# Keys' features turned by a trip through DRAM and VectorE's block transpose, and a linear attention's division moved to ScalarE

## The chip, the core and the metric

The kernel runs on one core of a Trainium2 chip. The core has TensorE (PE, with PEld for its weight loads), VectorE (DVE), ScalarE (ACT), GpSimd (POOL) and SyncE (SP), which here issues the DMAs, and 16 DMA engines. The metric is the time of one execution on the device in microseconds (us), as a median over runs. Everything is computed in 32-bit floats.

## What is computed

The input is 16 images of 56 x 56 tokens with 128 channels. There are two layers.

```
x = x + window_attention(group_norm(x))       # shifted windows of 7x7, 4 heads of 32
t = tokens(x)                                 # 16 x 3136 x 128
t = t + linear_attention(layer_norm(t))
t = t + recurrent(layer_norm(t))              # y_t = sigmoid(Wx_t + y_(t-1) V^T)
```

The change lies in the linear attention, which is causal over the 3136 tokens of an image:

```
q, k, v = split(x @ W.T + b);  q = elu(q) + 1;  k = elu(k) + 1
num_t = q_t . sum over s <= t of (k_s outer v_s)
den_t = q_t . sum over s <= t of k_s + 1e-6
out_t = num_t / den_t
```

The recurrence normalises over all images together before it starts, so it begins when everything else is done.

## The kernel before

**Stages.** The first stage, from the start to about 1538 us, does the window attention, the linear attention and the recurrence's input projection of all images. The second runs the recurrence, cut into 32 segments per image.

**Tiles.** An image is eight rows of windows (`window_row`, L830) and seven token groups (`token_group`, L1200): six full groups of 512 tokens in four chunks of 128, and one of 64. That makes 128 rows, 96 full groups and 16 small ones.

**A full group's linear attention.** The layer norm's scale is applied by GpSimd (L1101). The scaled tokens are then turned, channels to partitions, by a trip through DRAM (`through_dram`, L1045): SP issues one write of 256 KB (L1050) and four reads of 64 KB (L1057) into one of four buffers of tag "xp", and VectorE turns blocks of 32 x 32 (L1129). This is done for key "a" (linear attention) and key "f" (recurrence), for all images but the last. TensorE projects to the features of keys and queries (L1259), ScalarE and VectorE make the elu (L1269, L1278, L1287), channels on partitions. The values come out with tokens on partitions (L1312, L1321). The keys' features `f1` are needed in both forms. As they are they enter the products of keys and queries (L1375, masked by L1385). With tokens on partitions, `k`, they enter the running state, so TensorE transposes them chunk by chunk into a PSUM bank (L1335) and ScalarE copies them out (L1339).

**State.** For each chunk TensorE adds keys times values to a PSUM bank that holds the running sums (L1415), and ScalarE copies it (L1427). A chunk's result is queries times the state before it (L1404) plus the masked products times the values (L1407), in a pair of PSUM banks, with the divisor as the last column. VectorE takes the reciprocal of the divisors (L1477, L1480) and does one multiply-add per chunk onto the residual `xt_buf` (L1484). The result is stored (L1184) and goes on to the second layer norm.

**What sets the order.** Every piece of work is a step with an engine, a cost, a rank and the buffers that it takes and drops (`Plan`, L57). A list scheduler simulates all steps, forwards and backwards in 200 passes, keeps the order with the shortest simulated span, and emits the instructions in it. Each engine, and SP as the queue of the DMAs, then works through its own instructions in that order, and semaphores do the waiting. A changed step gives a new order of the whole stage. Buffers that matter here: three PSUM banks "b", two PSUM pairs "a", four buffers "xp", one each of "f0" and "f1", two of "k", three of "state".

**Dormant code.** With `KEYS = ('f', 'a')` (L30) `blocks_moved("k", ...)` (L1041) is false, so the branch at L1354, the strided writes at L1343 and the strided reads at L1350 are not used before the change.

Of the kernel before, what the change touches and what calls it, by code (L numbers as in the profile page):

```python
# [11 lines left out]
AF = mybir.ActivationFunctionType  # L12
ALU = mybir.AluOpType
# [13 lines left out]


TOL2 = 2.0 ** -38
KEYS = ('f', 'a')  # L30


class Buf:
# [201 lines left out]
def tile_conv_attn_hybrid(  # L235
# [19 lines left out]
    nc = tc.nc  # L255
    B, H, W, C = x.shape
    P = 128
# [4 lines left out]
    G = 4  # L262
# [165 lines left out]
    with ExitStack() as s1:  # L428
# [75 lines left out]
        for xt in xt_bufs:  # L504
# [22 lines left out]
                "f1": 1,  # L527
                "k": 2,
                "A": 1,
                "state": 3,  # L530
            }
        )
# [32 lines left out]
        s = issued = plan.step("SP", 0.1, -1.0, lambda: None, lag=19.0)  # L565
# [80 lines left out]
        def part(g, full, mini):  # L646

            return full if g < NG - 1 else mini
# [392 lines left out]
        def blocks_moved(key, b, g):  # L1041

            return key in KEYS and b < B - 1 and g < NG - 1

        def through_dram(key, b, g, src, xp, rank, after, drops):  # L1045

            there = xn_d[key][b, g]

            def away():
                nc.sync.dma_start(  # L1050
                    there.rearrange("s p r -> p s r"),
                    src().rearrange("p (s r) -> p s r", s=4),
                )

            def back():
                for s4 in range(4):
                    nc.sync.dma_start(  # L1057
                        at_spare(xp)[32 * s4 : 32 * (s4 + 1)].rearrange(
                            "i (q r) -> i q r", q=4
                        ),  # L1060
                        there[s4].rearrange("(q i) r -> i q r", q=4),
                    )
# [137 lines left out]
        def token_group(b, g, i, t, turned_x, rows_done, oT_buf, xt_buf, rank):  # L1200


            n = f"{b}_{g}"
            d, df = {}, {}
            st = plan.step
            v1 = v_bufs[i % 2]
            t0, t1 = group_tokens(g)
            nt = t1 - t0
            xg = chunks_of(g, t["xt"])
            np, nk, _ = xg.shape  # L1210
# [21 lines left out]
            def plus_attention():  # L1232
# [10 lines left out]
                takes=[bo],  # L1243
                drops=[oT_buf],
# [4 lines left out]
            xo, scaled = layer_scale(t, g, d, "a", rank, [s], xnT)  # L1249
# [3 lines left out]
            def feature(j):  # L1253
                key = f"f{j}"
                bp, r, f = Buf("b"), Buf("r"), Buf(key)

                def proj():
                    d[f"p{j}"] = bank(bp, P, nt)
                    nc.tensor.matmul(  # L1259
                        d[f"p{j}"],  # L1260
                        awc_sb[:, j * P : (j + 1) * P],
                        d["xT"][:, :nt],
                        start=True,
                        stop=True,
                    )

                def relu():
                    d[f"r{j}"] = own(r, P, GT)[:, :nt]
                    nc.scalar.activation(  # L1269
                        d[f"r{j}"],  # L1270
                        d[f"p{j}"],
                        AF.Relu,
                        bias=bqk_neg[:, j : j + 1],
                        scale=-1.0,
                    )

                def expo():
                    nc.scalar.activation(d[f"r{j}"], d[f"r{j}"], AF.Exp, scale=-1.0)  # L1278

                def larger():  # L1280
                    d[key] = own(f, P, GT)
                    to, a1, a2 = d[key][:, :nt], d[f"p{j}"], d[f"r{j}"]
                    if j and blocks_moved("k", b, g):
                        to = to.rearrange("p (c k) -> p k c", k=G)
                        a1 = a1.rearrange("p (k c) -> p k c", k=G)
                        a2 = a2.rearrange("p (k c) -> p k c", k=G)
                    nc.vector.scalar_tensor_tensor(  # L1287
                        to,
                        a1,
                        bqk_one[:, j : j + 1],  # L1290
                        a2,
                        ALU.add,
                        ALU.max,
                    )
# [10 lines left out]
            def chunk(f, cc):  # L1305
                return f[:, CK * cc : CK * (cc + 1)]
# [41 lines left out]
            def keys(cc):  # L1348
                if blocks_moved("k", b, g):
                    return d["f1"].rearrange("p (c k) -> p k c", k=G)[:, cc]  # L1350
                return chunk(d["f1"], cc)

            bk, k, bA, A = Buf("b"), Buf("k"), Buf("b"), Buf("A")
            if blocks_moved("k", b, g):  # L1354
# [17 lines left out]
            def products():  # L1372
                d["pA"] = bank(bA, P, nk, np)
                for cc in range(nk):
                    nc.tensor.matmul(  # L1375
                        d["pA"][:, cc, :],
                        keys(cc),
                        chunk(d["f0"], cc)[:, :np],
                        start=True,
                        stop=True,  # L1380
                    )
# [97 lines left out]
                d["rd"] = rd[:np, 0:na, 0:ni]  # L1479
                nc.vector.reciprocal(d["rd"], den)  # L1480

            def update():
                for cc in range(nk):
                    nc.vector.scalar_tensor_tensor(  # L1484
                        xg[:, cc, :],
                        d["pn4"][:, cc // 2, cc % 2, 0:C],
                        d["rd"][:, cc // 2, cc % 2 : cc % 2 + 1],
                        xg[:, cc, :],
                        ALU.mult,
                        ALU.add,  # L1490
                    )
# [498 lines left out]
```

## Time and profile before

| | before |
|---|---|
| median of 3 runs | 1694.72 us (1693.42 to 1697.08) |
| the profiled execution | 1699.48 us |
| its span, first to last instruction | 1697.7 us |
| granted TensorE clock, mean | 0.992 |
| recurrence, from about 1538 us on | 160 us |
| DMA packets | 539117, of them 208960 under 512 bytes |

The profile is a page of sections and answers to questions about the trace. Busy time is time in which an engine works, its share is of the span. The chain of work that ended last follows the last instruction back to what released it, step by step. A row of a group reads: line, engine, operation, written tile <- read tiles, shapes, count | busy us, mean ns of one | idle time just before, and what ended it. A DMA's landing is the time from its issue to its last semaphore. Matmuls are pipelined and their ends are modelled, so their durations overlap.

The DMA issues of the trips through DRAM in the page, with KB each and median us to landing:

```profile
xna_d<-spare SPq DMA_DIRECT2D x90, 256.0 KB, 2.5
spare<-xna_d SPq DMA_DIRECT2D x360, 64.0 KB, 2.0
xnf_d<-spare SPq DMA_DIRECT2D x90, 256.0 KB, 2.3
spare<-xnf_d SPq DMA_DIRECT2D x360, 64.0 KB, 2.1
```

The first of each pair is the write and the second the four reads, 90 groups each.

### The profile page before, as it was taken

Reading aid. Unit: us, or ns where it says so; the run is one execution under the profiler, and the core shown is the slowest. Engines: PE = TensorE matmul, PEld = TensorE weight load, DVE = VectorE, ACT = ScalarE, POOL = GpSimd, SP = SyncE. Lnnn points to the kernel's source line nnn. Section 1 sums busy time; section 2 is a strip of 40 time slices with the busy share of each in tenths; the row PEclk is TensorE's granted clock in tenths of the full one; section 3 lists DMA queues with packets and bytes.
Section 4 is the critical chain, followed back from the end, with each engine's and each line's share of the span. In section 5 each row is a group of like instructions: output and inputs, shape, how many; then the busy total and the mean of one; then the engine's idle time right before and its main releaser. Section 6 shows DMA issues by size and latency. Waiting matters only on the chain.

```text
span 1697.7 us, 63511 instructions
## 1 busy us (share of the span) xinstructions
PE 1651.5 (97%) x25819; PEld 1348.0 (79%) x25819; DVE 1444.7 (85%) x3354; ACT 1139.0 (67%) x2846; POOL 1152.5 (68%) x2042
## 2 busy tenths in 40 slices
PE   7999999999999999999999999999999998999997
PEld 6778878888887888888888888888787887786875
DVE  5889988898979898988988898989788876777997
ACT  5667667667676676766766767667666675666765
POOL 6788778688778687877876887787676765651000
PEclk9999999999999999999999999999999999999998
DMA  5465646364545547463746365545543343558999
GB/s 134 102 161 122 173 126 170 103 163 135 154 132 139 129 119 186 116 167 107 182 116 159 114 141 157 151 124 131 143 121 96 102 140 95 163 175 325 405 418 378
DMA packets 539117, 274.81 MB, mean 162 GB/s; under 512 B 208960, under 2 KB 522560, under 8 KB 537024
## 3 DMA queue, kind: packets, MB, share of 16 engines
q1 hardware_dynamic: 537232, 269.89, 54.5%
q8 instruction: 204, 3.34, 0.8%
q10 hardware_dynamic: 1584, 0.79, 0.2%
q14 instruction: 97, 0.79, 0.1%
HBM read 147.94 MB, written 122.65 MB: 159 GB/s over the span
## 4 chain that ended last, share of the span: by engine, by line
PE 81%; DVE 7%; POOL 4%; DMA 3%; issue 3%; SPq 1%; ACT 1%; DVEq 0%; POOLq 0%; ACTq 0%
PE bank L1259 9%; PE bank L857 9%; PE bank L878 6%; PE pair L902 6%; PE pair L957 5%; PE state_bank L1415 5%; PE pair L1404 5%; PE pair L1407 5%; PE pair L976 5%; PE bank L1312 5%; PE bank L1375 5%; PE bank L1224 5%; PE bank L1502 4%; DVE z_buf L1773 3%; PE z_buf L1785 3%
## 5 line engine op out<-in xcount | busy, mean ns | idle before, releaser
L928 POOL TENSOR_TENSOR s<-s,mx 128x784 f32<-128x784 f32 x128 | 192.4, 1503 | 84.9 <-DVE mx L925 82.3
L947 POOL TENSOR_TENSOR p_buf<-p_buf,rc 128x784 f32<-128x784 f32 x128 | 194.6, 1521 | 80.4 <-DVE rc L944 39.7
L1259 PE MATMUL bank<-xnT,awc_sb 128*128 128x512 f32 (+1 forms) x448 | 211.2, 554 | 4.6 <-DVE xt_buf L1233 3.4
L1269 ACT ACTIVATE r<-bank,bqk_neg 128x512 f32<-128x512 f32 (+1 forms) x224 | 142.7, 637 | 101.0 <-PE bank L1259 84.6
L1404 PEld LDWEIGHTS pair<-state,f 128*128 128x128 f32 x768 | 126.1, 191 | 53.5 <-issue 35.9
L1287 DVE SCALAR_TENSOR_TENSOR f<-bank,bqk_one,r 128x512 f32<-128x512 f32 (+1 forms) x224 | 147.6, 659 | 23.2 <-ACT r L1278 10.7
L1407 PE MATMUL pair<-v_buf,A 128*128 128x129 f32 x800 | 155.4, 276 | 0.8 <-issue 0.4
L967 ACT COPY pT<-pair 128x904 f32<-128x904 f32 x128 | 118.1, 923 | 54.6 <-PE pair L957 42.4
L1415 PEld LDWEIGHTS state_bank<-v_buf,k 128*128 128x128 f32 x768 | 123.7, 192 | 38.9 <-issue 21.0
L1415 PE MATMUL state_bank<-v_buf,k 128*128 128x129 f32 x768 | 153.8, 282 | 0.5 <-ACT state L1427 0.2
L1427 ACT COPY state<-state_bank 128x129 f32<-128x129 f32 x384 | 105.2, 274 | 72.7 <-PE state_bank L1415 69.9
L1404 PE MATMUL pair<-state,f 128*128 128x129 f32 x768 | 152.1, 280 | 0.0
L913 DVE TENSOR_TENSOR s<-pair,wmask_sb 128x784 f32<-128x784 f32 x128 | 122.9, 960 | 32.0 <-PE pair L902 27.8
L942 DVE TENSOR_REDUCE sm<-p_buf 128x16 f32<-128x784 f32 x128 | 121.9, 952 | 21.3 <-ACT p_buf L938 21.1
L1213 POOL TENSOR_TENSOR xt_buf<-xt_buf,bout_sb 128x512 f32<-128x512 f32 (+1 forms) x112 | 129.3, 1159 | 14.2 <-DMA xt_buf<-in_x_dram 13.9
L1788 ACT ACTIVATE y_a<-z_buf,bsh 128x256 f32<-128x256 f32 (+1 forms) x218 | 103.3, 474 | 45.5 <-PE z_buf L1785 41.5
L1278 ACT ACTIVATE r<-r 128x512 f32<-128x512 f32 (+1 forms) x224 | 130.7, 584 | 2.5
L902 PEld LDWEIGHTS pair<-kT,q_buf 32*49 32x49 f32 x8192 | 106.3, 121 | 32.3 <-issue 16.3
L1785 PE MATMUL z_buf<-y_a,fvT_sb 128*128 128x256 f32 (+1 forms) x432 | 129.7, 385 | 0.5 <-ACT y_a L1788 0.4
L902 PE MATMUL pair<-kT,q_buf 32*49 32x49 f32 x8192 | 122.6, 206 | 4.8 <-issue 4.8
L957 PEld LDWEIGHTS pair<-ident,p_buf 113*128 113x128 f32 x1024 | 108.1, 142 | 21.6 <-issue 9.6
L1407 PEld LDWEIGHTS pair<-v_buf,A 128*128 128x128 f32 x800 | 121.8, 192 | 3.9 <-issue 1.9
(162 smaller groups left out, 4619.0 us busy)
## 6 DMA issues: line engine op xcount, KB each, us to landing
x_d<-xt_buf SPq DMA_DIRECT2D x96, 256.0 KB, 2.5
xt_buf<-in_x_dram SPq DMA_DIRECT2D x93, 256.0 KB, 3.4
spare<-in_x_dram SPq DMA_DIRECT2D x60, 392.0 KB, 4.7
xs_d<-staged SPq DMA_DIRECT2D x15, 1568.0 KB, 7.0
xna_d<-spare SPq DMA_DIRECT2D x90, 256.0 KB, 2.5
spare<-xna_d SPq DMA_DIRECT2D x360, 64.0 KB, 2.0
xnf_d<-spare SPq DMA_DIRECT2D x90, 256.0 KB, 2.3
spare<-xnf_d SPq DMA_DIRECT2D x360, 64.0 KB, 2.1
```

What stands on the lines that cost most here:

```text
L857: nc.tensor.matmul(d[key], wqkv_sb[:, j * P : (j + 1) * P], xk, start=True, stop=True)
L902: nc.tensor.matmul(sc[64 * hh : 64 * hh + WT, hp, w * WT : (w + 1) * WT], qT[r : r + HD, w * WT : (w + 1) * WT], d["kT"][r : r + HD, w * W ...
L928: nc.gpsimd.tensor_tensor(d["sf"], d["sf"], d["mx"].unsqueeze(2).to_broadcast([P, nb, WT]), ALU.subtract,)
L947: nc.gpsimd.tensor_tensor(prf, prf, d["rc"].unsqueeze(2).to_broadcast([P, nb, WT]), ALU.mult)
L957: nc.tensor.transpose(pt[:, hp, w2, 0:NQ2], pr[0:NQ2, hp, 2 * w2 : 2 * w2 + 2, :].rearrange("p w k -> p (w k)"), ident[0:NQ2, 0:NQ2],)
L1259: nc.tensor.matmul(d[f"p{j}"], awc_sb[:, j * P : (j + 1) * P], d["xT"][:, :nt], start=True, stop=True,)
L1269: nc.scalar.activation(d[f"r{j}"], d[f"p{j}"], AF.Relu, bias=bqk_neg[:, j : j + 1], scale=-1.0,)
L1287: nc.vector.scalar_tensor_tensor(to, a1, bqk_one[:, j : j + 1], a2, ALU.add, ALU.max,)
L1404: nc.tensor.matmul(to, chunk(d["f0"], cc), t["states"][c], start=True, stop=False)
L1407: nc.tensor.matmul(to, d["A"][:, cc, :], v1[:, cc, :], start=c == 0, stop=True)
L1415: nc.tensor.matmul(t["pd"], d["k"][:, cc, :], v1[:, cc, :], start=c == 0, stop=True, skip_group_check=True,)
L1785: nc.tensor.matmul(z, fvT_sb, y_prev, start=False, stop=True, skip_group_check=True)
```

## The change

Two things are changed together.

**Keys.** "k" joins `KEYS`. For 15 images' full groups the keys' features go from `f1` to DRAM and come back. One write stores the tile `f1` (channels on partitions) as four chunks, each 128 x 128. Then four reads, one per quarter of 32 token places, bring for each of 32 partitions 16 runs of 32 numbers, 128 bytes each. VectorE's block transpose then reads and writes the 128 x 512 tile in plain order. The four TensorE transposes and ScalarE's copy of these groups go, and so does their PSUM bank. The strided forms of the dormant code go too.

**Division.** ScalarE multiplies the four chunks by their reciprocals out of PSUM into a new tile `at`. VectorE adds `at` to the residual in one instruction over the group. The pair of PSUM banks is dropped by ScalarE's step instead of VectorE's.

```
-KEYS = ('f', 'a')
+KEYS = ('f', 'a', 'k')
...
+                "at": 1,
...
+            runs = there.rearrange("s (q i) r -> i (s q) r", q=4)
...
             def back():
                 for s4 in range(4):
+                    to = at_spare(xp)[32 * s4 : 32 * (s4 + 1)]
+                    if key == "k":
+                        to = to.rearrange("i (n c) -> i n c", c=32)
+                        part = runs[:, :, 32 * s4 : 32 * (s4 + 1)]
+                    else:
+                        to = to.rearrange("i (q r) -> i q r", q=4)
+                        part = there[s4].rearrange("(q i) r -> i q r", q=4)
+                    nc.sync.dma_start(to, part)
...
             def turn_blocks():
                 d["k"] = own(k, P, G, C)
-                nc.vector.transpose(
-                    d["k"].rearrange("p k (q c) -> p k q c", q=4),
-                    at_spare(xp).rearrange("p (q c k) -> p k q c", q=4, k=G),
-                )
+                nc.vector.transpose(d["k"].rearrange("p k c -> p (k c)"), at_spare(xp))
...
+            def divided():
+                d["at"] = own(at, P, G, C)[:np, :nk]
+                for cc in range(nk):
+                    nc.scalar.activation(
+                        d["at"][:, cc, :],
+                        d["pn4"][:, cc // 2, cc % 2, 0:C],
+                        AF.Copy,
+                        scale=d["rd"][:, cc // 2, cc % 2 : cc % 2 + 1],
+                    )
+
             def update():
-                for cc in range(nk):
-                    nc.vector.scalar_tensor_tensor(
-                        xg[:, cc, :],
-                        d["pn4"][:, cc // 2, cc % 2, 0:C],
-                        d["rd"][:, cc // 2, cc % 2 : cc % 2 + 1],
-                        xg[:, cc, :],
-                        ALU.mult,
-                        ALU.add,
-                    )
+                nc.vector.tensor_tensor(xg, xg, d["at"], ALU.add)
...
-            up = st("DVE", part(g, (1.04, 1.12), (0.26, 0.34)), rank, update, [s, scaled], drops=[apn])
+            at = Buf("at")
+            s = st("ACT", part(g, (0.90, 1.00), (0.22, 0.32)), rank, divided, [s], takes=[at], drops=[apn])
+            up = st("DVE", part(g, (0.60, 0.69), (0.20, 0.28)), rank, update, [s, scaled], drops=[at])
```

More of the change, by code (lines that the diff above doesn't have):

```diff
@@ L1056, in back @@
                 for s4 in range(4):
[L1057 to L1061, printed above, removed]
-                    )
+                    to = at_spare(xp)[32 * s4 : 32 * (s4 + 1)]
[6 more added lines that the diff above has]
+                    nc.sync.dma_start(to, part)
             s = plan.step("SP", 0.7, rank, away, after, drops=drops, lag=2.6)
@@ L1281, in larger @@
                     d[key] = own(f, P, GT)
[L1282 to L1286, printed above, removed]
                     nc.vector.scalar_tensor_tensor(
-                        to,
-                        a1,
+                        d[key][:, :nt],
+                        d[f"p{j}"],
                         bqk_one[:, j : j + 1],
-                        a2,
+                        d[f"r{j}"],
                         ALU.add,
@@ L1342, in turn_blocks @@
                 d["k"] = own(k, P, G, C)
-                nc.vector.transpose(
-                    d["k"].rearrange("p k (q c) -> p k q c", q=4),
-                    at_spare(xp).rearrange("p (q c k) -> p k q c", q=4, k=G),
-                )
[L1348 to L1351, printed above, removed]
+                nc.vector.transpose(d["k"].rearrange("p k c -> p (k c)"), at_spare(xp))
             bk, k, bA, A = Buf("b"), Buf("k"), Buf("b"), Buf("A")
@@ L1376, in products @@
                         d["pA"][:, cc, :],
-                        keys(cc),
+                        chunk(d["f1"], cc),
                         chunk(d["f0"], cc)[:, :np],
@@ L1480, in divisors @@
                 nc.vector.reciprocal(d["rd"], den)
-            def update():
-                for cc in range(nk):
-                    nc.vector.scalar_tensor_tensor(
-                        xg[:, cc, :],
-                        d["pn4"][:, cc // 2, cc % 2, 0:C],
-                        d["rd"][:, cc // 2, cc % 2 : cc % 2 + 1],
-                        xg[:, cc, :],
-                        ALU.mult,
-                        ALU.add,
-                    )
+            def divided():
[7 more added lines that the diff above has]
+                    )
+            def update():
+                nc.vector.tensor_tensor(xg, xg, d["at"], ALU.add)
             s = st("DVE", (0.29, 0.37), rank, divisors, pns)
-            up = st("DVE", part(g, (1.04, 1.12), (0.26, 0.34)), rank, update, [s, scaled], drops=[apn])
+            at = Buf("at")
+            s = st("ACT", part(g, (0.90, 1.00), (0.22, 0.32)), rank, divided, [s], takes=[at], drops=[apn])
+            up = st("DVE", part(g, (0.60, 0.69), (0.20, 0.28)), rank, update, [s, scaled], drops=[at])
             store(b, g, t, up, xt_buf, rank)
```

## The prediction

> **What bounds the kernel now.** I read the page first: the engines' shares, then the chain of work that ended last.
>
> ```profile
> PE 1651.5 (97%) x25819; PEld 1348.0 (79%) x25819; DVE 1444.7 (85%) x3354; ACT 1139.0 (67%) x2846; POOL 1152.5 (68%) x2042
> ...
> PE 81%; DVE 7%; POOL 4%; DMA 3%; issue 3%; SPq 1%; ACT 1%; DVEq 0%; POOLq 0%; ACTq 0%
> ```
>
> TensorE is the busiest engine and holds 81% of the chain; VectorE is next, ScalarE and GpSimd have about a third free. The table by stretches then separates the attention stage (16 to 1538 us) from the recurrence behind it, where GpSimd is nearly idle and the DMA engines are full.
>
> ```profile
> 400.00:700.00 300.00, 298.96 (x5053) 245.79 (x5052) 263.01 (x637) 208.12 (x532) 230.55 (x405) 1.00 0.52 139
> 700.00:1000.00 300.00, 298.83 (x5041) 244.82 (x5040) 263.72 (x634) 205.99 (x523) 232.54 (x409) 1.00 0.54 139
> 1300.00:1538.00 238.00, 228.14 (x3411) 187.19 (x3411) 180.50 (x455) 152.75 (x392) 149.54 (x297) 0.99 0.42 135
> 1538.00:1697.70 159.70, 144.66 (x833) 114.11 (x831) 140.49 (x231) 104.24 (x220) 2.63 (x7) 0.97 0.96 387
> ```
>
> Columns: stretch, length, busy time of PE, PEld, DVE, ACT, POOL, granted clock, DMA share, GB/s. In steady state TensorE is hardly ever idle by this table and VectorE is busy for 88% (263.7 of 300). The change touches only the attention stage. Last, the chain itself, in a stretch around 706 us:
>
> ```profile
> 706.21 0.86 PE bank L1259 x2
> 707.07 0.44 PE bank L1335 x4
> 707.51 0.89 PE bank L1224 x8
> 708.40 0.22 PE pair L1404 x2
> 708.63 0.22 PE pair L1407 x2
> ```
>
> One TensorE step follows the other without a hole, and the four transposes of the keys (L1335) take 0.44 us of it. But the chain is not TensorE everywhere. Near 764 us it runs through a trip to DRAM:
>
> ```profile
> 763.74 1.00 POOL spare L1101
> 764.74 0.03 POOL ld_f L1087
> 764.76 4.14 DMA xna_d<-spare
> 768.90 0.02 issue
> 768.92 0.32 SPq L1057
> ```
>
> So TensorE sets the pace, with exceptions at just the kind of trip of which the change makes more.
>
> **The change, part by part.** Full groups of 512 tokens number 96 (16 images by 6); 90 of them (all but the last image's) send their keys through DRAM.
>
> TensorE loses the four transposes. The chain gives 0.44 us for them, so 90 x 0.44 = 39.6 us, nearly all of it on the path. The group's row has more:
>
> ```profile
> L1335 PE MATMUL bank<-ident,f 128*128 128x128 f32 x384 | 58.5, 274 | 1.9 <-issue 1.9
> L1339 ACT COPY k<-bank 128x512 f32<-128x512 f32 x96 | 56.7, 590 | 25.0 <-PE bank L1335 24.5
> L1484 DVE SCALAR_TENSOR_TENSOR xt_buf<-pair,rd,xt_buf 128x128 f32<-128x128 f32 x384 | 106.1, 339 | 1.1
> L1129 DVE STREAM_TRANSPOSE xnT<-spare 128x512 f32<-128x512 f32 x90 | 63.2, 702 | 14.8 <-DMA spare<-xna_d 12.3 <-PE bank L1259 2.0
> ```
>
> 58.5 us busy over 96 groups is 0.61 us each; the sum by it would be 54.9 us. I take 0.44, because the next step starts that much later (707.07 to 707.51) and the busy time overlaps it. The Trainium skill (Perfetto Trace Analysis, Identifying the Most-Contended Engine) calls matmul busy time a bad measure of how near TensorE is to its limit, since matmuls are pipelined. That agrees with 0.61 beside 0.44 here, and is a warning that the 97% holds small holes. By it the gain would be at most 39.6 us.
>
> ScalarE loses the copy out of PSUM, 90 x 0.59 = 53 us, and gains four scaled copies of 128x128 per full group. That form isn't in the trace; the nearest are the state copy (128x129 from PSUM, 0.274 us) below and the 128x392 scaled copy of the queries (L862, 0.501 us) above. At 0.274 it is 96 x 1.10 = 105 us, plus 16 small groups at about 0.25 = 4 us; at 0.501 it is 196 us. I take the former, whose shape is the same. Net +56 us on an engine busy 1028 us of the stage's 1522: 71%. Nothing, as long as the planner fits them in.
>
> VectorE loses four multiply-adds per group (106.1/96 = 1.11 us) and gains one addition of 128x512: 0.678 us by the residual after the window attention (L1233), 0.692 us by the one scaling with everything in SBUF (L1109). It also gains the block transpose: 0.702 us by L1129, which walks its tile in strides, 0.617 us by the 128x448 of the image (L676), 0.705 for 512 columns. Per group with keys moved: -1.11 + 0.69 + 0.70 = +0.28 us, 90 of them +25; the other six groups -0.42 each, the small ones about nothing. Net +22 us on 1296: VectorE goes from 85% of the stage to 87%, or 88% of a stage 22 us shorter. The row hides it in VectorE's own idle time; without that cover it costs up to 22 us.
>
> The PSUM bank of the transposed keys is freed for about 1 us per group (0.44 + 0.59). TensorE's waits at L1335 itself come to 8.1 us, at L1224 for the keys' copy to 2.2 us. This gain I bound by 0 and 10 us and leave it out of the sum.
>
> DMA and SP gain one write of 256 KB and four reads of 64 KB in 90 groups. The diff's reads are of 32 numbers, 128 bytes: 4 x 512 packets. Two short windows of the DMA view give the price of each kind:
>
> ```profile
> DMA packets 2752, 0.35 MB, mean 141 GB/s; under 512 B 2752, under 2 KB 2752, under 8 KB 2752
> ...
> q1 hardware_dynamic: 2752, 0.35, 88.8%
> ```
>
> This is an image's load in 128-byte runs, 814.0 to 816.5 us: 0.888 x 2.5 us x 16 engines / 2752 = 12.9 ns a packet. At 1425.0 to 1427.5 us a store in 512-byte runs had 481 packets and 32.4%: 26.9 ns. So the keys' read takes 2048 x 12.9 / 16 = 1.65 us of all 16 engines, where the layers' reads take 512 x 26.9 / 16 = 0.86, and the write 0.86 as well. 90 x 2.51 = 226 us on top of 0.51 x 1522 = 776: the DMA share of the stage goes from 51% to 66%. The Trainium skill (DMA: Bandwidth & Descriptors, Specifications) speaks against this part: it wants runs of at least 512 bytes for full rate. The rows show the loss, 1.9 times the time per byte, but at 66% there is still room for it.
>
> SP issues five more DMAs per group: 0.38 us for the write (L1050's median) and 4 x 0.43 (L1057's) = 2.1 us. At each read SP also waits for the write's landing; the queue's own waits give 122.2 + 88.8 = 211 us for the 180 trips of now, 1.17 us each. Together 3.3 us per group, 295 us more. Behind it in SP's order stand the next group's layer trips, the stores and the image loads. The issues at their medians now come to 720 x 0.43 + 180 x 0.38 + 112 x 0.38 + 109 x 0.46 + 60 x 0.50 = 501 us (layer reads, layer writes, stores, loads, image loads), with the landing waits 712, so SP is held 47% of the stage, after the change 66%.
>
> The moved keys come later. Now: 0.44 + 0.59, about 1.0 us after VectorE's maximum. Then: the write's landing 2.5 us, four issues 1.7, the last landing 2.0, transpose 0.7: 6.9 us. The groups come every 1522/96 = 15.9 us, so a planned order can cover the 5.9 us; the single buffers of the two feature tiles and the state chain (L1415, L1427, L1404) bound how far. What waits is VectorE at the block transpose, with everything behind it. Today's 180 transposes waited 24.2 + 12.3 = 36.5 us for their data, 0.20 us each. 90 more at that price are 18 us; at twice the price, because the queues are fuller and the layers' trips lengthen too, 36 us; wholly covered, 0. I take 18, next to the only rows there are.
>
> The planner makes the whole order anew. Of the stage's chain some 206 us are not TensorE (1522 less 81% of 1697.7 plus the 59 us that the recurrence's chain spends on TensorE). A tenth of it either way, 20 us, is my estimate for a luckier or unluckier order.
>
> **Sum.** -39.6 + 18 = -21.6 us. The profiled execution took 1699.48 us, with a span of 1697.7; it lies 4.8 us above the median of 1694.72. So 1677.9 us against its own time and **1673 us** against the median.
>
> **The rivals.**
> 1. All of TensorE's time comes back and the freed bank adds its part: -40 to -50 us, 1645 to 1655. For it: the gapless chain, ScalarE's free third. Against: the 0.20 us per transpose are already seen.
> 2. VectorE becomes the bound, or the reordering eats the gain: -39.6 + 18 + 22 = 0, 1685 to 1702. For it: 88% busy and waits in order. Against: its idle time of 12% is more than the 22 us.
> 3. Slower: the DRAM trips set the pace. One group's three trips share SP; when the keys' part (3.3 us of issue and landing wait) stands before the next layer trip on the chain, that trip is 3.3 us late, as at 764 us where a write of 2.5 us took 4.14. It decides from 39.6 / 3.3 = 12 of the 90 groups on; in 18 groups it costs 59 us and gives 1695 - 40 + 59 = 1714. For it: the chain has trips of 4 us today, and SP goes to 66%. Against: they are few, DMA and SPq being 4% of the chain (68 us).
> That the change does nothing of what it says is out: the transposes do leave TensorE.
>
> **How the numbers follow.** Forecast 0.42, between 1656 and 1690. Rival 1: 0.15. Rival 2: 0.17, a half of it within 0.2% (1691.3 to 1698.1), which is about what a measurement of this kernel can tell from no change, the rest 0.05 faster and 0.04 slower. Rival 3: 0.26. So faster 0.42 + 0.15 + 0.05 = 0.62, same 0.08, slower 0.30. The range reaches from rival 1's low end, 1645, to rival 3 in 18 groups, 1715.
>
> **What would show it.** Right: L1335 and L1339 with only 24 transposes and 6 copies left; TensorE's chain share as high as now in a stage of about 1500 us; the transpose of the keys near 0.70 us, waiting some 20 us for its DMA; VectorE near 88%, DMA share near 0.66 in the steady state. Wrong: TensorE with visible holes that end at L1415 or behind a block transpose; writes to DRAM landing in 4 us instead of 2.5; many more DMA and SPq pieces in the chain; four scaled copies that take far more than 1.1 us and hold the pair of PSUM banks.

## The result: 3.2% slower, and the profile after

The changed kernel takes 1750.05 us (median of 4 runs, 1743.08 to 1753.03) against 1694.51 us before on the same chip: a ratio of 1.032 [1.0287, 1.0352], so 55.5 us more. The forecast was 21.6 us less. The profiled execution took 1750.3 us with a span of 1748.5. Line numbers are those of the changed kernel: L1052 writes a trip's data to DRAM, L1066 reads them back, L1342 is the keys' block transpose, L1133 that of the two layers' tokens, L1406 the product of values and keys into the running sums, L1476 ScalarE's scaled copies, L1484 VectorE's addition. In the kernels that change the keys alone, the numbers around these are lower by one.

The engines' shares and the chain of work that ended last, of the kernel after:

```profile
PE 1644.4 (94%) x25459; PEld 1316.7 (75%) x25459; DVE 1482.2 (85%) x3156; ACT 1188.8 (68%) x3156; POOL 1172.6 (67%) x2042
...
PE 29%; DVE 23%; DMA 20%; SPq 11%; POOL 9%; issue 6%; ACT 2%; DVEq 0%; POOLq 0%
SPq L1066 10%; DMA spare<-xnk_d 5%; DMA xnk_d<-f 4%; PE bank L1263 3%; DMA xna_d<-spare 3%; PE bank L858 3%; DMA spare<-xnf_d 2%; DVE xt_buf L1484 2%; DMA xnf_d<-spare 2%; PE z_buf L1780 2%; PE bank L879 2%; POOL p_buf L948 2%; DVE z_buf L1768 2%; PE bank L1311 2%; DVE f L1286 2%
```

The engines' busy shares hardly moved, so none of them became a bound. The chain is a different one: TensorE fell from 81% to 29%, and DMA with SP's queue rose from 4% to 31% (542 us of 1748.5). The second line names them: the reads back (L1066) and all three trips, `xnk_d` of the keys, `xna_d` and `xnf_d` of the layers.

The stretches of the kernel after (columns: stretch, length, busy PE, PEld, DVE, ACT, POOL, granted clock, DMA share, GB/s):

```profile
400.00:700.00 300.00, 285.77 (x4586) 229.16 (x4590) 259.81 (x570) 204.61 (x555) 223.69 (x386) 0.98 0.66 167
700.00:1000.00 300.00, 285.48 (x4766) 229.16 (x4766) 261.51 (x563) 208.48 (x566) 226.33 (x388) 0.99 0.68 169
...
1590.00:1748.50 158.50, 143.84 (x829) 113.75 (x828) 139.23 (x228) 103.27 (x218) 2.62 (x7) 0.97 0.96 388
```

TensorE now idles for 14 us of 300 where it idled for 1, and does fewer instructions in the same time. VectorE is no busier. The DMA share is 0.66 to 0.68, as forecast. The recurrence is as long as before, so all of the loss lies in the attention stage, which ends near 1590 us instead of 1538.

What VectorE waited for, in the kernel after (us in total, times, longest):

```profile
DVE k L1342 <- DMA spare<-xnk_d: 70.2, 47, 3.9
DVE xfT L1133 <- DMA spare<-xnf_d: 29.0, 23, 3.8
DVE xnT L1133 <- DMA spare<-xna_d: 19.0, 20, 2.4
```

The forecast gave the keys' transposes 18 us of such waits. They took 70.2, or 0.78 us for each of 90; the layers' waits rose as well, from 36.5 to 48.0. Since each engine works in order, VectorE's idling passes on: TensorE's product with the keys (L1406) waited 21.6 us for L1342.

What SP, the issuing queue, waited for in the kernel after:

```profile
SPq L1052 <- POOL spare L1105: 121.3, 49, 26.1
SPq L1188 <- DVE xt_buf L1484: 113.2, 39, 10.7
SPq L1066 <- DMA xnk_d<-f: 70.0, 46, 3.6
SPq L1066 <- DMA xnf_d<-spare: 56.0, 44, 3.6
SPq L1066 <- DMA xna_d<-spare: 54.1, 39, 3.1
SPq L1052 <- DVE f L1286: 47.7, 30, 6.8
```

The first two lines are waits for tiles that GpSimd (scaled tokens) and VectorE (the residual to store) have not finished; they were larger before, 282.3 and 138.8 us. The others are of two kinds: for a write to land before it is read back, 180.1 us, and, new, for the keys' features before they can be written, 47.7 us. The landing waits are no larger in sum than the 211 us before, so their sum can't be what costs. What changed is that three trips now share the queue, so that a wait for one can hold up the other two. SP's order of issues around 780 us in the kernel after shows it (start, us, line, written <- read; four reads are merged):

```profile
775.70 1.05 SPq L1052 DMA_DIRECT2D xnk_d<-f  x1
776.80 1.36 SPq L1052 DMA_DIRECT2D xna_d<-spare  x1
...
781.86 5.00 SPq L1066 DMA_DIRECT2D spare<-xnk_d  x4
786.91 0.49 SPq L1052 DMA_DIRECT2D xnf_d<-spare  x1
787.50 0.45 SPq L1052 DMA_DIRECT2D xnk_d<-f  x1
787.99 2.04 SPq L1066 DMA_DIRECT2D spare<-xna_d  x4
```

The keys' write is issued at 775.70 and lands at 781.8. The reads of the keys stand for it, then take 5.00 us to issue instead of about 2. The layer's write of 776.80 is read back only at 787.99, and the next keys' write and another layer's stand behind as well. The plan counts on the keys 6.2 us after their write begins, here at 781.9, when the reads have just begun. This stretch of the chain says the same:

```profile
775.70 6.10 DMA xnk_d<-f
781.86 3.41 SPq L1066
```

Last, the changed groups of the kernel after (busy us, mean ns of one | idle before, and what ended it):

```profile
L1484 DVE TENSOR_TENSOR xt_buf<-xt_buf,at 128x512 f32<-128x512 f32 x96 | 96.7, 1007 | 6.3 <-ACT at L1476 6.2
...
L1342 DVE STREAM_TRANSPOSE k<-spare 128x512 f32<-128x512 f32 x90 | 63.6, 706 | 71.4 <-DMA spare<-xnk_d 70.2 <-issue 0.3
```

```profile
L1476 ACT ACTIVATE at<-pair,rd 128x128 f32<-128x128 f32 x384 | 110.2, 377 | 23.1 <-DVE rd L1471 22.3 <-PE pair L903 0.6
```

The block transpose costs what the forecast said, 0.706 us. The addition takes 1.007 us on average, not 0.69. ScalarE's copies take 0.377 us each, but overlap: 110.2 us over 384 are 0.287, close to the 0.274 of the forecast.

### The profile page after: what moved, and what is told of

It is laid out like the page before. It is cut to its first block, busy times and chain, and to the rows that moved or that the text cites. A ratio compares the mean times of both kernels' runs of the same rounds, so it can differ in the third digit from the quotient of the medians.

```text
span 1748.5 us, 63630 instructions
## 1 busy us (share of the span) xinstructions
PE 1644.4 (94%) x25459; PEld 1316.7 (75%) x25459; DVE 1482.2 (85%) x3156; ACT 1188.8 (68%) x3156; POOL 1172.6 (67%) x2042
## 4 chain that ended last, share of the span: by engine, by line
PE 29%; DVE 23%; DMA 20%; SPq 11%; POOL 9%; issue 6%; ACT 2%; DVEq 0%; POOLq 0%
SPq L1066 10%; DMA spare<-xnk_d 5%; DMA xnk_d<-f 4%; PE bank L1263 3%; DMA xna_d<-spare 3%; PE bank L858 3%; DMA spare<-xnf_d 2%; DVE xt_buf L1484 2%; DMA xnf_d<-spare 2%; PE z_buf L1780 2%; PE bank L879 2%; POOL p_buf L948 2%; DVE z_buf L1768 2%; PE bank L1311 2%; DVE f L1286 2%
## 5 line engine op out<-in xcount | busy, mean ns | idle before, releaser
L1263 PE MATMUL bank<-xnT,awc_sb 128*128 128x512 f32 (+1 forms) x448 | 215.0, 562 | 13.7 <-DVE xnT L1133 7.9
L1406 PEld LDWEIGHTS state_bank<-v_buf,k 128*128 128x128 f32 x768 | 124.8, 192 | 76.3 <-issue 29.4
L1406 PE MATMUL state_bank<-v_buf,k 128*128 128x129 f32 x768 | 157.9, 287 | 24.0 <-DVE k L1342 21.6
L1476 ACT ACTIVATE at<-pair,rd 128x128 f32<-128x128 f32 (+1 forms) x400 | 116.0, 376 | 23.3 <-DVE rd L1471 22.5
L939 ACT ACTIVATE p_buf<-s 128x784 f32<-128x784 f32 x128 | 112.8, 882 | 22.7 <-POOL s L929 22.3
L1366 PEld LDWEIGHTS bank<-f,f 128*128 128x128 f32 x800 | 102.0, 193 | 31.6 <-issue 12.3
```

Source lines behind the costliest of these rows:

```text
L1263: nc.tensor.matmul(d[f"p{j}"], awc_sb[:, j * P : (j + 1) * P], d["xT"][:, :nt], start=True, stop=True,)
L1406: nc.tensor.matmul(t["pd"], d["k"][:, cc, :], v1[:, cc, :], start=c == 0, stop=True, skip_group_check=True,)
```

## The experiments

Ratios stand with their 95% intervals, always against the kernel before on the same chip. The experiments ran on several chips, on which the kernel before took 1693.18 to 1698.51 us, so a difference between times of two chips is good to some 5 us.

### Which half costs what: keys alone, division alone, no trip

*Keys alone* is the changed kernel with the old multiply-adds on VectorE (L1484 of before); *division alone* is the changed kernel with one line undone:

```
-KEYS = ('f', 'a', 'k')
+KEYS = ('f', 'a')
```

The two without a trip let the block transpose read the features where they lie; their keys then stand in wrong places, and the work is otherwise the same. Here is the edit on keys alone; the whole change without a trip has the same one.

```
-                nc.vector.transpose(d["k"].rearrange("p k c -> p (k c)"), at_spare(xp))
+                nc.vector.transpose(d["k"].rearrange("p k c -> p (k c)"), d["f1"])
...
-                s = through_dram("k", b, g, lambda: d["f1"], xp, rank, [fk], [bfk])
+                s = fk
```

> The keys go through DRAM as in the change, but VectorE keeps its four multiply-adds per group (no division on ScalarE). Theory T (the keys' trip: SP's order and fuller DMA queues make VectorE wait at its block transposes, 118 us in the change against 36.5 before, and TensorE behind it): most of the loss is here, 1735 to 1755 us. Theory D (the division part: the one addition of two SBUF tiles took 1007 ns on average instead of 690, up to 3714): the trip is harmless and TensorE's 40 us come back in part, 1670 to 1700 us. Theory O (the planner found an unlucky order): no pattern between the parts.

> ScalarE divides and VectorE adds in one piece, but the keys are transposed by TensorE as before. T: 1690 to 1700 us, as before. D: 1720 to 1745 us, VectorE's addition of 128x512 again near 1000 ns. O: anything within some 20 us of before.

> The change with the keys' trip through DRAM left out: VectorE's block transpose reads the features' tile directly, so each 32x32 block is turned in place and the keys of the state are in wrong places; everything else, division on ScalarE included, is as in the change. T: the gain that was forecast appears, 1650 to 1680 us. D: the loss stays, 1720 to 1750 us, less TensorE's part. O: no statement.

> As the run before it, trip left out (keys of the state in wrong places), but also without the division part: TensorE without the keys' transposes, VectorE with one more block transpose per group, nothing else. T: 1650 to 1675 us. D: 1650 to 1675 us as well; the difference to the run with the division is the price of the division when no trip disturbs, 0 to 10 us by T, 30 to 50 by D.

| | us | ratio |
|---|---|---|
| keys alone | 1731.15 | 1.0229 [1.0192, 1.0265] |
| division alone | 1704.46 | 1.0072 [1.0049, 1.0096] |
| whole change, no trip | 1680.18 | 0.9921 [0.9896, 0.9947] |
| keys alone, no trip | 1650.50 | 0.9748 [0.9712, 0.9784] |

The kernel before took 1693.19 us beside these. Taking the transposes off TensorE, with VectorE's block transposes in, gives 42.7 us. The trip costs 1731.15 - 1650.50 = 80.7 us without the division and 1750.05 - 1680.18 = 69.9 with it. The division costs 11.3 us alone, 18.9 beside the trip, 29.7 without one. So both halves cost, and the trip far more; the division alone lies between the ranges of its two theories.

### Is it that the keys come late?

From here to the keys' own queue, all versions are made from keys alone. The trip is made in full, but the transpose reads `f1` and waits for no landing.

```
-            return plan.step("SP", 1.6, rank, back, [s], takes=[xp], lag=3.6)
+            return plan.step("SP", 1.6, rank, back, [s], takes=[xp], drops=[xp] if key == "k" else [], lag=3.6)
...
-                s = through_dram("k", b, g, lambda: d["f1"], xp, rank, [fk], [bfk])
+                through_dram("k", b, g, lambda: d["f1"], xp, rank, [fk], [bfk])
+                s = fk
```

> Keys only (VectorE keeps its multiply-adds); the keys' trip through DRAM is made in full, but VectorE's block transpose reads the features' tile and waits for no landing (keys of the state in wrong places). Between 1650 us (no trip) and 1731 (trip read). Theory Q (load: SP's issues and waits in order, fuller DMA queues, later trips of the layers): 1700 to 1730 us. Theory L (lateness of the keys: VectorE stands at its block transpose, the state and the buffers behind it): 1650 to 1670 us.

1739.75 us, 1.0251 [1.0228, 1.0273], no better than keys alone, and above both ranges. VectorE's waits in this kernel:

```profile
DVE xfT L1132 <- DMA spare<-xnf_d: 66.1, 35, 6.0
DVE xnT L1132 <- DMA spare<-xna_d: 37.4, 23, 3.6
```

Nobody waits for the keys, and the waits for the layers' trips are 103.5 us, where the kernel before had 36.5 and keys alone 32.2. So in this kernel it isn't enough that the keys be in time. But the edit changes what the planner knows, and with it the order; the pair with one order comes below.

### Is it the DMA engines, by the short runs or the bytes?

*Long runs*: the keys are read in runs of 512 bytes, as the layers are (another order of the numbers in `k`). *Small trip*: one write and one read of 16 KB instead of five DMAs of 512 KB in all; the transpose reads the 32 columns that come back sixteen times.

```
-                    if key == "k":
-                        to = to.rearrange("i (n c) -> i n c", c=32)
-                        part = runs[:, :, 32 * s4 : 32 * (s4 + 1)]
-                    else:
-                        to = to.rearrange("i (q r) -> i q r", q=4)
-                        part = there[s4].rearrange("(q i) r -> i q r", q=4)
+                    to = to.rearrange("i (q r) -> i q r", q=4)
+                    part = there[s4].rearrange("(q i) r -> i q r", q=4)
```

```
+                    nc.sync.dma_start(there[0, :, 0:32], src()[:, 0:32])
...
+                    nc.sync.dma_start(at_spare(xp)[:, 0:32], there[0, :, 0:32])
...
+                s = plan.step("SP", 0.4, rank, away, after, drops=drops, lag=2.6)
+                return plan.step("SP", 0.4, rank, back, [s], takes=[xp], lag=3.6)
```

> Keys only, the keys read from DRAM in 512-byte runs as the layers' are, 512 packets a group in place of 2048; the numbers then land in wrong places of the tile, all else stays. Theory R (the short runs are what costs): half of the 80 us comes back, 1680 to 1705 us. Q: the DMA share falls by some 5 points, SP stays, 1715 to 1730. L: the landing is little sooner, 1722 to 1732.

> Keys only, with a trip that carries a sixteenth: one write and one read of 16 KB instead of one of 256 KB and four of 64 KB, and the block transpose reads the 32 columns that come back sixteen times (so the keys of the state are wrong). The wait for two landings stays, SP has 3 issues less, the DMA engines nearly no load from it. Q: 1655 to 1680 us. L: 1700 to 1730 us. R: as Q.

Long runs: 1732.60 us, 1.0216 [1.0189, 1.0243], the same as keys alone, though the DMA share of 100 to 1300 us fell from 0.68 to 0.64. The run length isn't it. Small trip: 1724.18 us, 1.0160 [1.0133, 1.0188], at a share of 0.53, that of the kernel before. That speaks against the bytes and lies in the range of theory L, but this kernel gives the planner other costs and so has another order; taken alone it is inconclusive.

### Is the planned order bad, or its execution?

The planner gets the whole trip; no DMA of the keys is issued, and the transpose reads `f1`. The order on TensorE, VectorE, ScalarE and GpSimd is that of keys alone, which the two traces confirm.

```
-            s = plan.step("SP", 0.7, rank, away, after, drops=drops, lag=2.6)
-            return plan.step("SP", 1.6, rank, back, [s], takes=[xp], lag=3.6)
+            s = plan.step("SP", 0.7, rank, (lambda: None) if key == "k" else away, after, drops=drops, lag=2.6)
+            return plan.step("SP", 1.6, rank, (lambda: None) if key == "k" else back, [s], takes=[xp], lag=3.6)
```

> Keys only, with the trip in the plan and nowhere else: TensorE, VectorE, ScalarE and GpSimd run exactly the order of the keys-only run (1731 us), but SP issues none of the keys' five DMAs, and the block transpose reads the features' tile (keys of the state in wrong places). Theory O (the order that the planner makes with a third trip is bad as such: buffers, later keys): 1715 to 1730 us. Theory Q (the order is good, what is executed on SP and the DMA engines is late): 1655 to 1675 us.

1654.72 us, 0.9758 [0.9742, 0.9774]. Its chain:

```profile
PE 89%; DVE 6%; issue 2%; POOL 2%; ACT 0%; DMA 0%; SPq 0%; DVEq 0%; POOLq 0%; ACTq 0%
```

With the DMAs gone TensorE has 89% of the chain, and the same order runs in 76.4 us less than keys alone. So the order is good as long as its data come as planned; what costs is the execution of the keys' DMAs. VectorE's waits for trips, first with the DMAs (keys alone), then without them:

```profile
DVE k L1341 <- DMA spare<-xnk_d: 71.4, 51, 5.0
DVE xfT L1132 <- DMA spare<-xnf_d: 17.3, 17, 2.5
DVE xnT L1132 <- DMA spare<-xna_d: 14.9, 17, 1.7
```

```profile
DVE xfT L1132 <- DMA spare<-xnf_d: 7.1, 9, 1.4
DVE xnT L1132 <- DMA spare<-xna_d: 4.0, 6, 2.0
```

In one and the same order the keys' DMAs bring 71.4 us of waits for the keys and raise those for the layers from 11.1 to 32.2. So most of the waiting is for the keys themselves, and the other trips are delayed as well. In the fast version SP still waited 185.2 us for the layers' landings (110.8 and 74.4): waits of SP as such do not set the time.

### Late against what? The planned landing times

The planner lets the next step count on a write 2.6 us after its step begins and on the reads 3.6 us after theirs (`lag`). In the kernel after, a write's median landing is 2.6 to 3.0 us; three issues of 0.43 to 0.49 ahead of the last read and its landing of 2.0 to 2.2 make 3.3 to 3.7, before any wait in the queue. Medians alone fill the plan, and 70 of the 90 keys' trips issued their first read later than 2.6 us after the write. *Longer lags* are keys alone with 4.5 and 5.5 for all three trips. Then 6.0 and 7.0; then longer lags for the layers only.

```
-            s = plan.step("SP", 0.7, rank, away, after, drops=drops, lag=2.6)
-            return plan.step("SP", 1.6, rank, back, [s], takes=[xp], lag=3.6)
+            s = plan.step("SP", 0.7, rank, away, after, drops=drops, lag=4.5)
+            return plan.step("SP", 1.6, rank, back, [s], takes=[xp], lag=5.5)
```

> Keys only, correct, with the trips' planned times to landing raised from 2.6 to 4.5 us for the write and from 3.6 to 5.5 us for the reads, for all three keys, so that the planner leaves more room between issue and use. Theory M (the planned times are too short for what the queue does): 1690 to 1715 us instead of 1731. Theory Q0 (SP or the DMA engines are simply used up, no order helps): 1725 us or more.

> Keys only, correct, the planned times to landing of all three trips raised further, to 6.0 us for the write and 7.0 for the reads (4.5 and 5.5 gave 1678.6 us, 2.6 and 3.6 gave 1731). Theory M (only the room in the plan is missing): 1660 to 1680 us. If the buffers or SP's share of the time are the limit by now: 1680 to 1700 us.

> Keys only, correct, longer times for the two layers' trips alone, the keys' own trip planned with 2.6 and 3.6 us as in the change. If it is the layers' trips that come late behind the keys' (theory S, SP's order): 1680 to 1695 us, most of the way to 1678.6. If it is the keys' own landing that VectorE stands for (theory L): 1710 to 1730 us.

| lags of writes and reads | us | ratio |
|---|---|---|
| 2.6 and 3.6 (keys alone) | 1731.15 | 1.0229 [1.0192, 1.0265] |
| 4.5 and 5.5, layers only | 1718.50 | 1.0128 [1.0112, 1.0144] |
| 4.5 and 5.5 | 1678.64 | 0.9897 [0.9875, 0.9919] |
| 6.0 and 7.0 | 1689.44 | 0.9975 [0.9963, 0.9987] |

Two numbers of the plan, and no other line of the kernel, give back 52.5 of the trip's 80.7 us. The chain of 4.5 and 5.5, and VectorE's waits in it:

```profile
PE 65%; DVE 15%; DMA 6%; SPq 4%; issue 4%; POOL 3%; ACT 1%; DVEq 0%; POOLq 0%; ACTq 0%
```

```profile
DVE k L1341 <- DMA spare<-xnk_d: 17.5, 14, 3.9
...
DVE xfT L1132 <- DMA spare<-xnf_d: 7.9, 9, 1.5
```

All waits for trips shrink together, though nothing lands sooner: the writes' median landings are 3.1, 2.4 and 2.8 us (`xna_d`, `xnf_d`, `xnk_d`), against 2.7, 2.4 and 2.6 in keys alone. DMA and SP's queue fall to 10% of the chain, and the waits at the transpose of the keys to 17.5 us, about the 18 of the forecast. The DMA share of 100 to 1300 us is 0.71, the highest of all, in a kernel that is faster than before. So the mean load on the DMA engines was not the limit. With long lags for the layers only, the waits for the keys stay as in keys alone, and those for the layers shrink:

```profile
DVE k L1341 <- DMA spare<-xnk_d: 78.1, 55, 3.8
...
DVE xfT L1132 <- DMA spare<-xnf_d: 6.1, 5, 3.6
```

Room for the layers' trips alone gives 12.7 of the 52.5 us; the rest came only with room for the keys' trip as well. Long lags for the keys alone were not run. With 6.0 and 7.0 the kernel is slower than with 4.5 and 5.5, though its waits for trips are all but gone:

```profile
DVE k L1341 <- DMA spare<-xnk_d: 1.1, 2, 0.6
```

So what it loses lies elsewhere in the order; that it is the buffers, which are held for longer, is not shown.

### A queue of their own for the keys

The keys' five DMAs go to ScalarE's queue, planned as work of ScalarE.

```
+            queue = nc.scalar if key == "k" else nc.sync
+            on = "ACT" if key == "k" else "SP"
+            s = plan.step(on, 0.5, rank, away, after, drops=drops, lag=2.6)
+            return plan.step(on, 1.8, rank, back, [s], takes=[xp], lag=3.8)
```

> Keys only, correct, the keys' five DMAs issued by ScalarE's queue instead of SP's, the layers' trips as before on SP. Theory S (SP's order: waits for the features and for the landing stand before the layers' trips, stores and loads): the waits of the layers' transposes fall back to 36 us and the time to 1690 to 1715 us, unless ScalarE's own 2 us of issues per group eat that. Theory E (the DMA engines' load): 1725 us or more, with writes still landing in 2.8 to 3.0 us.

1862.60 us, 1.0974 [1.0953, 1.0996], by far the slowest. ScalarE also works in order, and waits for the keys' DMAs now stand before its copies out of PSUM, the largest of them before the copies of the state:

```profile
ACT state L1419 <- DMA spare<-xnk_d: 28.1, 9, 5.0
```

TensorE was busy for 1079.9 us of 100 to 1300, against 1153.1 in keys alone. Here an engine with other work was a worse place for such waits.

### The same lags on the kernel before, on the whole change, on the division

> The kernel before, keys on TensorE, with the planned times to landing of the layers' trips raised from 2.6 and 3.6 to 4.5 and 5.5 us: the control for the run at 1678.6 us. Theory M (the planned times fit a queue with two trips a group and not one with three): little to gain here, 1680 to 1696 us. Theory G (the longer times are worth the same anywhere, and the keys' trip still costs more than it gives): 1640 to 1665 us.

> The whole change with the same longer times. M: the loss of 55 us turns into about the keys-only run's gain less the division's price, 1680 to 1695 us. Q0 (SP and the DMA engines are used up by three trips and the division on top): 1715 us or more.

> Division part alone with the same longer times (1704.5 us without). Theory T (the division's loss too comes of trips that are planned too short, since the later residual starts them later): 1680 to 1695 us, no slower than the kernel before with the longer times. Theory H (the way VectorE, ScalarE, VectorE itself costs): 8 to 12 us over the kernel before with the longer times.

| 4.5 and 5.5 on | us | ratio |
|---|---|---|
| before | 1684.94 | 0.9937 [0.9923, 0.9951] |
| whole change | 1698.39 | 1.0011 [0.9995, 1.0026] |
| division alone | 1700.79 | 1.0031 [1.0020, 1.0041] |

The kernel before gains 0.6% by the lags too, 10.8 us. So of the fastest version's 1.0%, the keys' change itself has some 0.4%: 6.3 us, of 42.7 that its transposes are worth without a trip. The whole change with longer lags is no faster than before; the division costs it 19.8 us (1698.39 against 1678.64), and costs the kernel before with these lags 15.9.

### What the division costs

Three edits. *In PSUM*: ScalarE writes the divided chunks back to their PSUM pair and VectorE adds from there. *Measured costs*: division alone, planned with dearer steps. *Unread*: the kernel before with its multiply-adds, and ScalarE's four copies beside them, which nobody reads; they hold the PSUM pair too.

```
-                        d["at"][:, cc, :],
+                        d["pn4"][:, cc // 2, cc % 2, 0:C],
...
+                nc.vector.tensor_tensor(x4, d["pn4"][:, :, :, 0:C], x4, ALU.add)
```

```
+            s = st("ACT", part(g, (1.15, 1.30), (0.35, 0.45)), rank, divided, [s], takes=[at], drops=[apn])
+            up = st("DVE", part(g, (0.84, 0.93), (0.40, 0.48)), rank, update, [s, scaled], drops=[at])
```

```
+            at = Buf("at")
+            st("ACT", part(g, (0.90, 1.00), (0.22, 0.32)), rank, divided, [s], takes=[at], drops=[apn, at])
```

> Division part alone (keys turned by TensorE as before), but ScalarE writes the quotients back to the pair of PSUM banks and VectorE's one addition reads them there, so it has one operand in SBUF and one in PSUM instead of two in SBUF. Theory P (the addition of two SBUF tiles stands still while GpSimd works, 911 ns on average and up to several us in the run of the division part alone): the addition takes about 680 ns and never over 1 us, and the time goes from 1704 to 1680 to 1695 us. Theory H (the way over ScalarE itself costs: a later result, a longer held pair): 1700 to 1710 us, though the addition may be short.

> Division part alone, correct, with the plan's costs set to what the runs measured: the four scaled copies 1.15 us and 1.30 to the result (0.90 and 1.00 before), the addition 0.84 and 0.93 (0.60 and 0.69). Theory M (the loss of 11 us comes of an order made with too small costs): 1690 to 1697 us, as the kernel before. Theory H (the way over ScalarE costs in any order): 1700 to 1710 us.

> The kernel before, correct, and ScalarE makes the four scaled copies of the division part besides, which nobody reads: VectorE keeps its multiply-adds and waits for none of them. Theory A (ScalarE's 1.15 us more per group is what costs, its copies for TensorE come later): 1700 to 1712 us, as the division part alone (1704.5). Theory H (the hop: VectorE's addition waits for ScalarE): 1692 to 1698 us, as the kernel before.

| | us | ratio |
|---|---|---|
| division alone | 1704.46 | 1.0072 [1.0049, 1.0096] |
| in PSUM | 1708.93 | 1.0062 [1.0042, 1.0081] |
| measured costs | 1703.44 | 1.0046 [1.0029, 1.0062] |
| unread | 1733.07 | 1.0230 [1.0211, 1.0248] |

The addition, first of division alone, then of the version in PSUM:

```profile
L1484 DVE TENSOR_TENSOR xt_buf<-xt_buf,at 128x512 f32<-128x512 f32 x96 | 87.5, 911 | 20.2 <-ACT at L1476 19.6
```

```profile
L1484 DVE TENSOR_TENSOR xt_buf<-pair,xt_buf 128x512 f32<-128x512 f32 x96 | 65.7, 684 | 28.3 <-ACT pair L1474 27.8
```

With one operand in PSUM the addition is back at 0.684 us, so its excess does come from having both in SBUF; yet the time stays the same. That theory had the mechanism and not the loss. Neither the planned costs explain it, as the intervals overlap, nor trips that are planned too short, as the division costs 15.9 us with the longer lags too. The unread copies cost 39.9 us at once (1733.07 against 1693.18), more than the division itself. But in that run VectorE's multiply-adds waited 29.3 us, 43 times, behind ScalarE's copies, though they don't read them. So it did not take the hop between the engines away and separates nothing. What stays open is how the division's 11 to 30 us divide between the hop (VectorE to ScalarE to VectorE), ScalarE's 116 us of copies, the longer hold on the PSUM pair and the new order.

## Why the prediction was wrong

- **TensorE, -39.6 us: right in size.** Keys alone without the trip gave -42.7 us, near the 0.44 us of the chain and not the 0.61 of the busy time (54.9 us). That run also has VectorE's new transposes, the freed PSUM bank and an order of its own, so it doesn't measure the term by itself.
- **The waits at the keys' transposes, +18 us: this step failed.** They came to 70.2 us, 0.78 each, and the trip cost 70 to 81 us of time. I took the price of today's transposes, 0.20 us, "next to the only rows there are". That price belonged to a queue with two trips a group. It was no property of a transpose but of the slack between a planned landing and the real one: with longer lags the same waits fell to 17.5 and to 1.1 us. The two lag numbers stand in the step that plans a trip. Set beside the traced landings (2.3 to 2.5 us against a planned 2.6; 3 x 0.43 + 2.1 = 3.4 us against 3.6) they would have shown that a median trip had 0.1 to 0.3 us to spare, and one behind a waiting queue none.
- **SP held 66% of the stage, costed at nothing: the wrong measure.** I counted occupancy, and too much of it: the landing waits were 180.1 us for 270 trips, not 1.17 us each. What cost was lateness against the plan: 76.4 us between the same order with the keys' DMAs and without them. How much of the lateness is waits for other trips in the queue, how much slower issues and later landings, no run separates.
- **Rival 3 had a part of the mechanism**, trips on SP that set the pace, and the end of it: a chain with 31% DMA and SP. But it looked for the delay at the next layer trip. The waits for the layers rose by 11.5 us only; those for the keys' own data were 70.2. It set 18 groups without a source, so that its 59 us come near the measured 70 to 81 is luck. Its 1714 came out too low by that and by the division, for which it had nothing.
- **DMA share 66%: right, and no limit by itself**, as the version with 0.71 and 1678.64 us shows.
- **The division, put at nothing in ScalarE's free third: this step failed too.** ScalarE's busy sum was right (116.0 us against 109), but the division cost 11 to 30 us of time; through what is open. VectorE's addition was mis-sized, 96.7 us against 66, but that did not set the time.
- **The planner's order, 20 us either way: too small.** The same work ran in 1731.15, 1689.44 and 1678.64 us in the orders that three pairs of lags gave. The order of keys alone was a good one for the landings that it counted on and a bad one for the real landings; the prediction looked for luck where the plan had too little room.

By the runs the sum is -42.7 + 80.7 + 18.9 = 56.9 us, beside the measured 55.5.

## What to carry to other kernels

Before you add a DMA round trip to a kernel that is ordered by a plan, compare the plan's landing times with the traced ones; with several trips on one in-order queue, plan the wait as well, since a late landing can delay the trips behind it. Test such a loss by planning the trip and not issuing it, which tells in a single run whether the planned order or the execution of its DMAs costs. An engine at 68% has room in sum, but here the work that was moved onto it, on the way of a result, still cost 11 to 30 us.

## What the runs showed of the hardware

- **Runs of 128 bytes cost time on the DMA engines and none of the kernel's time here.** With the keys' reads in 512-byte runs the DMA share fell from 0.68 to 0.64 and the time stayed (1731.15 and 1732.60 us).
- **An addition with both operands in SBUF waited out the GpSimd instruction that was at work when it started.** In the kernel after its median was 0.686 us, the mean of the full groups 1.007 and the longest 3.714; with one operand in PSUM the mean was 0.684. One of the long ones, with GpSimd's instruction beside it (start, us):

```profile
733.61 1.50 POOL L929 TENSOR_TENSOR s<-s,mx 128x784 f32<-128x784 f32 x1
733.95 1.71 DVE L1484 TENSOR_TENSOR xt_buf<-xt_buf,at 128x512 f32<-128x512 f32 x1
```

  GpSimd's instruction ends at 735.11 and the addition 0.55 us later. So it is in all of them: 43 of the 96 full additions took over 0.8 us, each of these began while a GpSimd instruction was at work, and 40 ended 0.54 to 0.58 us after that instruction; the other three waited out the next ones too. Of the 53 short ones 18 began so as well, most beside the small instructions (128x4 numbers) of the layer norm's statistics. With one operand in PSUM 58 of 96 began beside GpSimd's work and none took over 0.693 us. The Trainium skill (SBUF — State Buffer, SBUF: two separate sides) says that VectorE and GpSimd share a pair of ports under an exclusive lock, which a VectorE operation with two SBUF inputs takes against a GpSimd operation that reads SBUF, for a whole instruction. The rows agree with it; no run here took GpSimd's work away.
- **Issuing a DMA has no fixed price.** In the stretch shown, four reads of 64 KB took SP 5.00 us where about 2 were usual, and single writes 1.05 and 1.36 where 0.45 and 0.49 follow. Over the whole run one such read took 0.30 to 3.53 us, in the kernel before 0.30 to 3.37. What slows an issue is not shown.
